# The local branch of a Mamba block: turned by transfers within SBUF, and projected by one matmul in place of four

## The chip, the cores and the metric

The kernel runs on one core of a Trainium2 chip, in one launch. The metric is device time in microseconds. Engines are named as in the profile: PE is TensorE (PEld its weight loads), DVE is VectorE, ACT is ScalarE, POOL is GpSimd, SP is SyncE, which in this kernel issues DMAs and nothing else. All data are 32-bit floats.

## The reference

The input is 32 images of 128 channels and 56 x 56 pixels. Layer 0 is a 7x7 depthwise convolution with a mixture of eight experts behind it. Layer 1, which the change touches, has a local and a global branch:

```python
xh = einsum('oi,bihw->bohw', cv1_w, x) + cv1_b
l  = depthwise_conv3x3(xh, dw_w)
l  = silu((l - bn_m) * (bn_g / sqrt(bn_v + 1e-5)) + bn_b)      # local branch, 128 channels
t  = layernorm_over_channels(tokens(xh))
g  = mamba(t)      # in_proj, causal conv, scan over 256 channels x 16 states, gate, out_proj
out = einsum('oi,bihw->bohw', cv2_w, concatenate([l, g], axis=1)) + cv2_b
return x + out
```

`cv2_w` is 128 x 256: its first 128 input channels take the local branch `l`, the others the global branch `g`.

## The kernel before

Layer 1 works on chunks of 448 pixels (8 image rows; seven chunks per image, 224 in all, numbered `g`). Within a chunk, the 16 states of the scan are 16 units. For each unit, GpSimd multiplies `du` by a broadcast row of B (`db_pool`, L1331), ScalarE makes the decay (`exp_act`, L1344), VectorE runs the scan over 2 x 449 columns (`scan_dve`, L1362 and L1366), VectorE or GpSimd multiplies by a broadcast row of C (`cmul`, L1382), and TensorE adds the product up in PSUM (`sum_pe`, L1285).

The rows of B and C (`bb` and `cb`) are loaded by `bc_load` (L1325), two units at a time and broadcast to 128 partitions, from a small DRAM tile `bc_d`, which `px_act` has stored there (L1189). `bb` and `cb` have three buffers each. All loads and stores of the layer are issued by SP, in one order.

That order, like that of every engine, is written out by hand. The table `PLAN` has a key for each step of a chunk and `UNITS` for each step of a unit. A key is a place in time counted in units, relative to the chunk's (or the unit's) own start; chunk `g` starts at 16 g. All steps of all chunks are sorted by key and emitted in that order, and each engine works through its own part of the list. A step can thus stand among the steps of the chunk before or after.

The local branch goes like this. `lt_pe` makes the 3x3 convolution in two PSUM tiles: TensorE works in 64 x 64 quarters, so channels 64 r to 64 r + 63 are in tile r, and within a tile the partitions 64 k to 64 k + 63 hold half k of the chunk's 448 columns. `lt_act` (L1266, keys -3.032 and -2.343) applies the batch norm and writes `lt`, 128 partitions x 2 (r) x 224 columns. `lt_silu` (L1171, key 2.033) applies SiLU in place. Much later `out_pe` (key 23.328, so among the steps of the next chunk) makes the output in one PSUM tile `p_out`: the residual `x1` through the identity (L1301), the local branch with `cvlt` (L1305), and the global branch with `wo` (L1311). Since `lt` has its channels spread over r and the partition half, `cvlt` is kept as four 128 x 128 matrices, one for each k and r, in which the half of the rows that belongs to the other k is zero; four matmuls over 224 columns each take the place of one plain one. `out_act` (L1316) and a store `out<-ot` follow.

`weights` loads all weights of layer 1 while layer 0 still works.

Of the kernel before, what the change touches and what calls it, by code (L numbers as in the profile page):

```python
# [5 lines left out]
F32 = mybir.dt.float32  # L6
# [7 lines left out]
C = 128  # L14
# [20 lines left out]
CH1 = L // NQ1  # L35
TPC1 = CH1 // TT
HD = 64
# [51 lines left out]
    (-2.343, "lt_act", 1),  # L89
    (2.033, "lt_silu"),  # L90
    (3.656, "dd_pe"),
    (18.599, "yz_dve", 0),
    (18.857, "yz_dve", 1),
    (23.328, "out_pe"),
# [150 lines left out]
def tile_kernel(tc: tile.TileContext, a: dict, out: bass.AP):  # L245
    nc = tc.nc
# [13 lines left out]
    with (  # L260
# [15 lines left out]
        for k in (HW - 1, 3 * HW - 1):  # L276
            nc.gpsimd.affine_select(
                out=perm, in_=perm, compare_op=ALU.not_equal, fill=1.0, base=-k, pattern=[[1, TT]],
# [7 lines left out]
        def column(v, name):  # L286
            t = const.tile([v.shape[0], 1], F32, name=name)
            nc.sync.dma_start(out=t, in_=v.unsqueeze(1))
            return t
# [185 lines left out]
        with (  # L475
# [9 lines left out]
            for k in range(0, E * CAP // 128, ZT):  # L485
# [6 lines left out]
                out=before, in_=ones[:, :128], compare_op=ALU.is_gt, fill=0.0, base=0,  # L492
# [7 lines left out]
            for q in range(QB):  # L500
                p = rp.tile([128, 3, TT], F32, name="p_turn", tag="tot", bufs=3)
# [61 lines left out]
            def total(v, first=None):  # L563

                p = rp.tile([128, v.shape[1]], F32, name="p_tot", tag="tot", bufs=3)
                if first is not None:
                    nc.tensor.matmul(p, lhsT=ones[:, :128], rhs=first, start=True, stop=False)
                nc.tensor.matmul(p, lhsT=ones[:, :128], rhs=v, start=first is None, stop=True)
                return p
# [22 lines left out]
            for h in range(2):  # L592
                p = total(cnts[h])
                r = room[:, h * HE : (h + 1) * HE]
# [33 lines left out]
            def chosen(i):  # L628
                t = tie[:, i, :]
                r = rs.tile([128, PT], F32, name="junk")  # L630
                nc.vector.tensor_tensor(
                    r.rearrange("j (r t) -> j r t", t=RUN), upto[:, i, :].rearrange("j (r t) -> j r t", t=RUN),
                    over[:, i, :].unsqueeze(2).to_broadcast([128, PT // RUN, RUN]), ALU.is_gt,
                )
                nc.vector.tensor_tensor(r, r, t, ALU.mult)
                nc.vector.scalar_tensor_tensor(
                    t, key[:, i, :], cands[i // HE][:, i % HE : i % HE + 1], r, ALU.is_gt, ALU.add
                )
                scan(i)
                return earlier(upto[:, i, PT - 1 : PT])  # L640
# [14 lines left out]
            p = chosen(0)  # L655
            for i in range(E):
                pn = chosen(i + 1) if i + 1 < E else None
                places(i, p)
                p = pn
# [15 lines left out]
        def weights(wp, wt, pw):  # L675
            def mm_tile(name):
                return pw.tile([128, 512], F32, name=name, tag="mm")
# [22 lines left out]
            dtt = wp.tile([128, DI], F32, name="dtt")  # L700
            nc.vector.memset(dtt, 0.0)
            nc.sync.dma_start(out=dtt[:DR], in_=a["dt_proj_wT"])
            cvlt = wp.tile([128, 2, 2, C], F32, name="cvlt")
            nc.gpsimd.memset(cvlt, 0.0)
            for k in range(2):
                nc.sync.dma_start(
                    out=cvlt[k * HD : (k + 1) * HD, k], in_=a["cv2_wT"][:C, :].rearrange("(r d) c -> d r c", r=2)
                )
            cv2b = column(a["L1_conv_cv2_b"], "cv2b")
            c1b3 = wp.tile([128, 2, 1], F32, name="c1b")  # L710
            turned(a["L1_conv_conv1d_b"].unsqueeze(1), c1b3)
# [41 lines left out]
            for h in range(2):  # L753
# [7 lines left out]
            p = mm_tile("p_mb")  # L761
# [11 lines left out]
                out=inp[:, 2:4, :], in_=a["L1_conv_in_proj_w"][DI:].rearrange("(h p) c -> p h c", p=128)  # L773
# [19 lines left out]
            p = mm_tile("p_ms")  # L793
# [8 lines left out]
            for k in range(DC + 1):  # L802
                p = mm_tile("p_wk")
                for h in range(2):
                    if k < DC:
                        s = wt.tile([128, C], F32, name="inx_s", bufs=2)
                        nc.vector.tensor_scalar_mul(s, inp[:, h, :], c1w[:, h, k : k + 1])
                    else:
                        s = inp[:, 2 + h, :]
# [5 lines left out]
            p = mm_tile("p_wo")  # L815
            for h in range(2):
                nc.tensor.matmul(
                    p[:, h * 128 : (h + 1) * 128], lhsT=wop[:, h * 128 : (h + 1) * 128], rhs=cvgt,
                    start=True, stop=True,
# [14 lines left out]
        with (  # L834
# [13 lines left out]
            for q in range(QB):  # L848
                for p0 in range(0, TT, XT):
                    ps = slice(p0, p0 + XT)  # L850
                    o = q * TT + p0
                    xgs = [dp.tile([128, XT, RW], F32, name=f"xg{k}") for k in range(2)]
                    nc.sync.dma_start(out=xgs[0][:, :, :C], in_=res_b[q, :, ps, :])
                    nc.scalar.copy(xgs[1][:, :, :C], xgs[0][:, :, :C])  # L854
                    for k, xg in enumerate(xgs):
                        nc.vector.tensor_copy(xg[:, :, C], gates[k][:, o : o + XT])  # L856
                        nc.vector.tensor_copy(xg[:, :, C + 1].bitcast(I32), backs[k][:, q, ps])
                        for j in range(XT):
                            apart(nc.gpsimd.indirect_dma_start(  # L859
                                out=buf_d[:, :],  # L860
                                out_offset=bass.IndirectOffsetOnAxis(ap=slots[k][:, o + j : o + j + 1], axis=0),
                                in_=xg[:, j, :], in_offset=None,
                            ), "scatter")
                if q == QB // 2:
                    w3 = weights(w3p, w3t, p3t)
# [5 lines left out]
        with (  # L871
# [8 lines left out]
                out=lsr, in_=a["L0_conv_layer_scale"].rearrange("c a b -> (c a b)").partition_broadcast(128)  # L880
# [47 lines left out]
            for e in range(E):  # L928
# [10 lines left out]
                for i0 in range(0, CAP, GT * 128):  # L939
# [3 lines left out]
                    for j, m, n in wholes(tiles):  # L943
                        r0 = e * CAP + i0 + j * 128
                        nc.sync.dma_start(
                            out=xb[:n, j:m, :],
                            in_=buf_d[r0 : r0 + (m - j) * n, :].rearrange("(k p) c -> p k c", p=n),
# [12 lines left out]
        with tc.tile_pool(name="p3", bufs=2, space=PSUM) as pmm:  # L960

            def mm_tile(name):
                return pmm.tile([128, 512], F32, name=name, tag="mm")

            layer1(w3 | locals())
# [3 lines left out]
def layer1(s):  # L969
# [3 lines left out]
    nc, tc, N = s["nc"], s["tc"], s["N"]  # L973
# [4 lines left out]
    st = [dict() for _ in range(G + 2)]  # L978
# [3 lines left out]
    with (  # L982
# [279 lines left out]
        def lt_act(g, r):  # L1262
            d = st[g]
            if r == 0:
                d["lt"] = two.tile([128, 2, CH1 // 2], F32, name="lt")
            nc.scalar.activation(  # L1266
                d["lt"][:, r, :], d["p_l"][r][:, : CH1 // 2], AF.Identity,
                bias=s["bnt"][:, r, 0:1], scale=s["bnt"][:, r, 1:2],
            )

        def yz_dve(g, h):
            d = st[g]
            if h == 0:
                d["yz"] = one.tile([128, 2, CH1], F32, name="yz")
            nc.vector.tensor_tensor(d["yz"][:, h, :], d["py"][:, h, :CH1], d["zs"][:, h, :], ALU.mult)
            if h == 1:
                del d["py"], d["zs"]
# [20 lines left out]
        def out_pe(g):  # L1298
            d = st[g]
            d["p_out"] = p = mm_tile("p_out")  # L1300
            nc.tensor.matmul(p[:, :CH1], lhsT=ident, rhs=d.pop("x1"), start=True, stop=False)  # L1301
            lt = d.pop("lt")
            for k in range(2):
                for r in range(2):
                    nc.tensor.matmul(  # L1305
                        p[:, k * CH1 // 2 : (k + 1) * CH1 // 2], lhsT=s["cvlt"][:, k, r, :], rhs=lt[:, r, :],
                        start=False, stop=False,
                    )
            yz = d.pop("yz")
            for r in range(2):  # L1310
                nc.tensor.matmul(p[:, :CH1], lhsT=s["wo"][:, r, :], rhs=yz[:, r, :], start=False, stop=r == 1)  # L1311
# [135 lines left out]
```

## Time and profile before

| | |
|---|---|
| median of 3 runs | 15727.1 us (15721.97 to 15732.7) |
| the profiled execution | 15731.48 us, of which its span is 15729.8 us |
| busy in the span: PE, PEld | 12850.2 us (82%), 7187.1 us (46%) |
| busy in the span: DVE, ACT, POOL | 11117.9 us (71%), 10499.4 us (67%), 13444.6 us (85%) |
| DMA | 2521.00 MB, mean 160 GB/s |

The span is the time from the first to the last instruction. Busy time is a mean over stages with different limits, so layer 1 has to be read by itself: it begins after about 5,700 us and lasts to the end. In a line of the timeline the first two numbers are the start in us from the span's start and the duration in us; a matmul of 32-bit floats leaves two records, each with its own weight load.

### The profile page before, as it was taken

Reading aid. Unit: us, or ns where it says so; the run is one execution under the profiler, and the core shown is the slowest. Engines: PE = TensorE matmul, PEld = TensorE weight load, DVE = VectorE, ACT = ScalarE, POOL = GpSimd, SP = SyncE. Lnnn points to the kernel's source line nnn. Section 1 sums busy time; section 2 is a strip of 40 time slices with the busy share of each in tenths; the row PEclk is TensorE's granted clock in tenths of the full one; section 3 lists DMA queues with packets and bytes.
Section 4 is the critical chain, followed back from the end, with each engine's and each line's share of the span. In section 5 each row is a group of like instructions: output and inputs, shape, how many; then the busy total and the mean of one; then the engine's idle time right before and its main releaser. Section 6 shows DMA issues by size and latency. Waiting matters only on the chain. (4 is left out here: it accounts for less than half of the span.)

```text
span 15729.8 us, 249821 instructions
## 1 busy us (share of the span) xinstructions
PE 12850.2 (82%) x92981; PEld 7187.1 (46%) x92981; DVE 11117.9 (71%) x11366; ACT 10499.4 (67%) x21038; POOL 13444.6 (85%) x8122
## 2 busy tenths in 40 slices
PE   7997200003999989999999999999999999999998
PEld 7996100002777754444444444444444444444443
DVE  2655500000111149999999999999999999999999
ACT  4564300001444458888888888888888888888887
POOL 2343377777888879999999999999999999999999
PEclk9997555556999999999999999999999999999999
DMA  8785422223555545555555555555555555555555
GB/s 264 231 234 167 186 78 78 78 78 69 71 70 72 70 106 183 184 185 182 182 184 182 183 184 184 181 183 182 183 184 183 181 184 183 182 185 185 179 183 167
DMA packets 1325298, 2521.00 MB, mean 160 GB/s; under 512 B 139352, under 2 KB 777136, under 8 KB 1316400
## 3 DMA queue, kind: packets, MB, share of 16 engines
q1 hardware_dynamic: 1127600, 2310.57, 47.2%
q0 software_dynamic: 196480, 194.45, 7.3%
q8 instruction: 732, 11.99, 0.3%
q14 instruction: 486, 3.98, 0.1%
HBM read 2129.06 MB, written 375.43 MB: 159 GB/s over the span
## 5 line engine op out<-in xcount | busy, mean ns | idle before, releaser
L1331 POOL TENSOR_TENSOR db<-du,bb 128x896 f32<-128x896 f32 x3584 | 6838.7, 1939 | 0.1
L1344 ACT ACTIVATE da<-dt,aneg 128x449 f32<-128x449 f32 x7168 | 4539.9, 637 | 389.1 <-DVE prod L1382 114.5
L1362 DVE TENSOR_TENSOR_SCAN da<-da,db 128x898 f32<-128x898 f32 x2240 | 4522.6, 2019 | 3.0 <-ACT da L1344 2.2
L1285 PE MATMUL py<-prod,ident 64*64 64x448 f32 x28672 | 3241.5, 548 | 174.6 <-DVE prod L1382 130.0
L1382 POOL TENSOR_TENSOR prod<-hs,cb 128x896 f32<-128x896 f32 x1344 | 2604.6, 1938 | 189.4 <-DVE r L1094 85.7
L1382 DVE TENSOR_TENSOR prod<-da,cb 128x896 f32<-128x896 f32 x2240 | 2438.7, 1089 | 199.0 <-DMA cb<-bc_d 85.2
L859 POOL DMA_INDIRECT buf_d<-xg,slot x1568 | 1515.4, 966 | 481.7 <-issue 453.9
L911 POOL DMA_INDIRECT res_d<-ys,xb x984 | 1587.8, 1614 | 332.3 <-issue 271.0
L1362 DVE TENSOR_TENSOR_SCAN hs<-da,db 128x898 f32<-128x898 f32 x896 | 1784.7, 2012 | 0.1
L1285 PEld LDWEIGHTS py<-prod,ident 64*64 64x64 f32 x28672 | 1018.0, 132 | 1628.2 <-issue 887.4
L951 PE MATMUL ept<-ident,xb 128*128 128x128 f32 (+1 forms) x984 | 188.7, 274 | 1916.7 <-DMA xb<-buf_d 1916.7
L1125 PE MATMUL p_xm<-te,wk 128*128 128x448 f32 x3584 | 1395.5, 540 | 0.0
L903 DVE TENSOR_TENSOR ys<-py,b2t 128x512 f32<-128x512 f32 (+2 forms) x256 | 170.7, 670 | 1690.5 <-PE py L897 1667.1
L856 DVE COPY xg<-gate 128x14 f32<-128x14 f32 x112 | 20.3, 184 | 1740.9 <-DMA buf_d<-xg,slot 1740.9
L854 ACT COPY xg<-xg 128x1792 f32<-128x1792 f32 x56 | 94.5, 1688 | 1684.3 <-DMA buf_d<-xg,slot 1673.4
L897 PEld LDWEIGHTS py<-w2t,hh 128*128 128x128 f32 x7872 | 936.2, 191 | 175.5 <-issue 113.4
L951 PEld LDWEIGHTS ept<-ident,xb 128*128 128x128 f32 (+1 forms) x984 | 124.6, 143 | 1920.1 <-issue 1919.8
L897 PE MATMUL py<-w2t,hh 128*128 128x128 f32 x7872 | 985.0, 278 | 0.3
L1125 PEld LDWEIGHTS p_xm<-te,wk 128*128 128x128 f32 x3584 | 671.5, 189 | 665.5 <-issue 567.1
L379 PE MATMUL pc<-xc,toep 112*112 112x112 f32 (+1 forms) x8192 | 944.9, 271 | 36.5 <-ACT toep L368 31.9
L1366 DVE TENSOR_TENSOR_SCAN hs<-da,db 128x449 f32<-128x449 f32 x896 | 926.2, 1076 | 1.4 <-ACT db L1390 0.8
L1257 PE MATMUL p_l<-xh,dwd 64*64 64x224 f32 x16128 | 907.1, 352 | 22.7 <-ACT dt L1239 4.2
(241 smaller groups left out, 20290.1 us busy)
## 6 DMA issues: line engine op xcount, KB each, us to landing
bb<-bc_d SPq DMA_DIRECT2D x1792, 448.0 KB
cb<-bc_d SPq DMA_DIRECT2D x1792, 448.0 KB
toep<-toep_d SPq DMA_DIRECT2D x448, 392.0 KB
buf_d<-zero SPq DMA_DIRECT2D x28, 2275.0 KB
xb<-buf_d SPq DMA_DIRECT2D x240, 260.0 KB
xt<-in_x SPq DMA_DIRECT2D x32, 1568.0 KB
res_d<-xa SPq DMA_DIRECT2D x128, 392.0 KB
xg<-res_d SPq DMA_DIRECT2D x56, 896.0 KB
```

The lines of the kernel that those rows point to most:

```text
L379: nc.tensor.matmul(pc[:, c, :, lo:hi], lhsT=tp[c // 2][:, c % 2, 6 - 2 * o : 8 - 2 * o, :], rhs=s4[:, c, :, lo + o - 1 : hi + o - 1], star ...
L859: apart(nc.gpsimd.indirect_dma_start(out=buf_d[:, :], out_offset=bass.IndirectOffsetOnAxis(ap=slots[k][:, o + j : o + j + 1], axis=0), in_ ...
L897: nc.tensor.matmul(py[:n, j, :], lhsT=hh[:, k, j * 128 : j * 128 + n], rhs=w2t[:, k, :], start=k == 0, stop=k == KF - 1,)
L911: apart(nc.gpsimd.indirect_dma_start(out=res_d[:, :], out_offset=bass.IndirectOffsetOnAxis(ap=xb[:n, j, C + 1 : C + 2].bitcast(I32), axis= ...
L1125: nc.tensor.matmul(p[:, :CH1], lhsT=s["wk"][:, k, hs], rhs=d["te"][:, k : k + CH1], start=k == 0, stop=k == DC - 1 and not first,)
L1257: nc.tensor.matmul(d["p_l"][r][k * HD : (k + 1) * HD, : CH1 // 2], lhsT=s["dwd"][rs, t, rs], rhs=d["xh"][rs, dy + k * R : dy + (k + 1) * R ...
L1285: nc.tensor.matmul(ps[r][h * HD : (h + 1) * HD, :CH1], lhsT=lhsT(rs, h), rhs=rhs[rs, h, :], start=start, stop=stop,)
L1331: nc.gpsimd.tensor_tensor(dbv[i][:, :, 1:], st[g]["du"], units[u].pop("bb"), ALU.mult)
L1344: e = nc.scalar.activation(da[:, h * W1 : (h + 1) * W1], st[g]["dt"][:, h, :], AF.Exp, scale=s["aneg"][:, h, i : i + 1])
L1362: nc.vector.tensor_tensor_scan(hs, da, dbs[i], 0.0, ALU.mult, ALU.add)
L1366: half(u, h, nc.vector.tensor_tensor_scan(hs2[h][:, hh], da[:, hh], dbs[i][:, hh], 0.0, ALU.mult, ALU.add))
L1382: eng.tensor_tensor(w["prod"], w["hs"][0][:, :, 1:], w["cb"], ALU.mult)
```

## The change

The step `lt_turn` is new, with key 5.0. Four DMAs, issued by SP, copy the quarters of `lt` into a new tile `lc` that has 128 channels as partitions and all 448 columns beside each other. `out_pe` then needs one matmul over 448 columns with the plain 128 x 128 `cvlt`. `lt` has one buffer in place of two; `lc` has two. The weight `cvlt` is loaded by one plain DMA, without a memset.

```diff
     (2.033, "lt_silu"),
     (3.656, "dd_pe"),
+    (5.0, "lt_turn"),
     (18.599, "yz_dve", 0),
...
-            cvlt = wp.tile([128, 2, 2, C], F32, name="cvlt")
-            nc.gpsimd.memset(cvlt, 0.0)
-            for k in range(2):
-                nc.sync.dma_start(
-                    out=cvlt[k * HD : (k + 1) * HD, k], in_=a["cv2_wT"][:C, :].rearrange("(r d) c -> d r c", r=2)
-                )
+            cvlt = load(a["cv2_wT"][:C, :], [C, C], "cvlt")
...
         def lt_act(g, r):
             d = st[g]
             if r == 0:
-                d["lt"] = two.tile([128, 2, CH1 // 2], F32, name="lt")
+                d["lt"] = one.tile([128, 2, CH1 // 2], F32, name="lt")
...
+        def lt_turn(g):
+            d = st[g]
+            lt = d.pop("lt")
+            lc = d["lc"] = two.tile([C, CH1], F32, name="lc")
+            for r in range(2):
+                for k in range(2):
+                    nc.sync.dma_start(
+                        out=lc[r * HD : (r + 1) * HD, k * CH1 // 2 : (k + 1) * CH1 // 2],
+                        in_=lt[k * HD : (k + 1) * HD, r, :],
+                    )
...
-            lt = d.pop("lt")
-            for k in range(2):
-                for r in range(2):
-                    nc.tensor.matmul(
-                        p[:, k * CH1 // 2 : (k + 1) * CH1 // 2], lhsT=s["cvlt"][:, k, r, :], rhs=lt[:, r, :],
-                        start=False, stop=False,
-                    )
+            lt = d.pop("lc")
+            nc.tensor.matmul(p[:, :CH1], lhsT=s["cvlt"], rhs=lt, start=False, stop=False)
```

`HD` is 64, `CH1` is 448 and `C` is 128. The lines of the profile before are those of the kernel before; in the changed kernel the matmul stands at L1310 and the new transfers at L1273.

## The prediction

> **What bounds the kernel now.** The diff touches the second layer, and beside that only a few instructions that run once, so I read the layer by itself: the windows view (columns: stretch and its length, then busy time and instruction count of each engine, granted TensorE clock, DMA share, GB/s).
>
> ```profile
> core 0: us, PE busy (x) PEld busy (x) DVE busy (x) ACT busy (x) POOL busy (x), PEclk, DMA share, GB/s
> 8000.00:10000.00 2000.00, 1908.12 (x14060) 895.80 (x14060) 1960.87 (x1530) 1729.96 (x3588) 1960.72 (x1049) 1.00 0.58 183
> ```
>
> VectorE and GpSimd are both busy 98% of the time and TensorE 95.4%. Ninety chunks pass in the 4000 us from 8000 to 12000 (90 `lt_silu` activations, L1171), so a chunk takes 44.4 us and 224 of them 9,950 us. Two engines at 98% can't both be read as the limit from busy time, so the waits come next, over the whole run (engine, line, what it waited for: us in total, times, longest). VectorE:
>
> ```profile
> DVE prod L1382 <- DMA cb<-bc_d: 85.2, 147, 2.1
> ...
> DVE yz L1275 <- PE py L1285: 4.0, 1, 4.0
> ...
> DVE prod L1382 <- PE p_var L1072: 3.1, 2, 1.6
> ```
>
> and GpSimd:
>
> ```profile
> POOL prod L1382 <- DVE r L1094: 85.7, 140, 1.1
> ...
> POOL prod L1382 <- DMA cb<-bc_d: 18.3, 30, 1.8
> POOL prod L1382 <- PE py L1285: 5.9, 28, 0.3
> ...
> POOL prod L1382 <- PE p_cv L1038: 4.0, 2, 2.1
> ```
>
> GpSimd waits once per chunk for VectorE (a scan whose product it takes; the named `r` stands beside it in VectorE's queue). Within the layer VectorE waits for other engines only in such single cases; what recurs is the load `cb`, 85.2 us in all. So VectorE with the `cb` loads sets the pace, and everything that TensorE ever makes these two wait is 4.0 + 3.1 + 5.9 + 4.0 = 17.0 us. Busy at 95%, TensorE is almost as full as the others and is still not waited for.
>
> Then the place of the change, in the timeline of SP's DMA queue in one chunk (start us, us, instruction). `lt_turn` (key 5.0) comes behind `px_act`'s store `bc_d<-xd` (16 - 11.507 = 4.493) and ahead of the next chunk's `bb` load of units 2 and 3 (18 - 11.504 = 6.496):
>
> ```profile
> 9008.09 1.79 SPq L1325 DMA_DIRECT2D cb<-bc_d  x2
> 9009.94 0.42 SPq L1189 DMA_DIRECT2D bc_d<-xd  x1
> 9015.23 0.32 SPq L1325 DMA_DIRECT2D bb<-bc_d  x1
> 9015.60 0.42 SPq L1015 DMA_DIRECT2D x<-in_x  x1
> 9016.08 0.43 SPq L1017 DMA_DIRECT2D yg<-res_d  x1
> 9020.90 0.32 SPq L1325 DMA_DIRECT2D cb<-bc_d  x1
> ```
>
> and all engines in the same microseconds:
>
> ```profile
> 9012.11 1.68 PE L1305 MATMUL p_out<-lt,cvlt 128*128 128x224 f32 x8
> ...
> 9012.57 2.01 DVE L1362 TENSOR_TENSOR_SCAN da<-da,db 128x898 f32<-128x898 f32 x1
> ...
> 9013.62 1.67 PE L1311 MATMUL p_out<-yz,wo 128*128 128x448 f32 x4
> ...
> 9014.67 1.09 DVE L1382 TENSOR_TENSOR prod<-da,cb 128x896 f32<-128x896 f32 x1
> ```
>
> The queue stands still from 9010.36 to 9015.23, 4.87 us, because `bb` reads what `bc_d<-xd` is still writing. The same place is also where VectorE is tightest: the product at 9014.67 needs the `cb` load issued at 9009.56, two DMAs ahead of the new ones. The trace's semaphore records put the landing of that load 4.43 us (median of 140 chunks; 3.2 to 6.5) after the issue of `bc_d<-xd`, about 9014.4; the scan ends at 9014.58. There is 0.2 us to spare.
>
> **The change, part by part.**
> *TensorE.* Four matmuls over 224 columns go: L1305 has 8 records (two per matmul), 1.68 us per chunk. One matmul over 448 columns comes; the row L1311 has two of exactly that shape, 1.67 us, so one is 0.83. TensorE loses 1.68 - 0.83 = 0.85 us per chunk, 190 us in all. What of that is on the path: at most the 17.0 us above, at least nothing; I take nothing, since those are single waits of 0.2 to 4 us and not a steady one. If all of it counted, the time would be 190 us less. At the end of the program `p_out` is in the chain that ended last, so the last chunk's 0.85 us count in full. The new matmul waits for four transfers issued 45 us before (`out_pe` of a chunk runs one chunk after its `lt_turn`).
>
> *SP's queue.* Four more issues per chunk, at 0.42 us as L1189, L1015 and L1017 (longest L1189 issue 1.43): 1.7 us, at most 5.7, beginning at 9010.4. The 4.87 us pause covers the first; past it, `bb`, `x`, `yg` and the next `cb` would shift, by 0.9 us at most. The `cb` at 9020.90 waits 4.4 us for GpSimd after `yg` is issued, so even that is covered. Their own waits are past: `lt_silu` ended at 9001.07, and the `lc` buffer was last read by the `out_pe` of 44 us ago. What the new ones are put ahead of is also used late: `bb` of units 2 and 3 by `db_pool` at key 15.71 (9.2 units of 44.4/16 = 2.78 us, 25 us, after its own key), `x` and `yg` by `moe_pe` 6.8 units (19 us) after theirs.
>
> *ScalarE.* `lt` has one buffer in place of two, so the next chunk's `lt_act` (9028.48) now waits for the transfers. Issued by 9012.1 and behind stores that land at 9014.6 (median; worst 9016.6), they should land by about 9017, with `out<-ot` (224 KB, 4.0 us) as nearest row. Ten us to spare: nothing. If that cover went, ScalarE would stand still with the next `exp_act` behind it, and VectorE after that.
>
> *DMA engines.* 4 x 56 KB = 224 KB more per chunk. A chunk moves 16 x 448 + 3 x 224 + 56 = 7,896 KB now, so 2.8% more. At 183 GB/s for a share of 0.58, the engines do 315 GB/s when busy, so 224 KB cost 0.73 us; with packets of 896 B in place of 3,584, I allow up to double, 1.46 us. That falls into the pause: after the `cb` load and `bc_d<-xd` have drained there is no other traffic until `bb` is issued. Does it slow the `cb` load ahead of it? In all 140 chunks no part of `bc_d<-xd` landed before the first part of that `cb` load, though it was issued 0.37 us later: what is issued later waits its turn. So I take nothing, and keep as upper end that the `cb` load is stretched by the whole 0.73 to 1.46 us. A gain here is excluded: no transfer is removed.
>
> There is a rule that speaks against the edit. The Trainium skill (SBUF — State Buffer, sections "Door 1: The DMA port swizzle" and "The DMA setup-cost knee") says that a transfer over 64 partitions reaches half of the SBUF ports, 196 GB/s against 328 at 1 MiB, that each transfer pays about 2 us, and that one transfer over 128 partitions should be used rather than several. No row here shows a 64-partition transfer between SBUF tiles. By the page's figures, and with the fixed parts one after the other, an estimate is 4 x 2 + 1.2 = 9.2 us per chunk, landing near 9020: beyond the pause, still 8 us before `lt_act`, and the sum would be the same.
>
> *Once per run.* A GpSimd memset of 0.6 us (L704) and one of two weight DMAs go, in a stage where GpSimd issues scatters: -0.6 us at most.
>
> *Sum.* The profiled execution took 15731.5 us (span 15729.8 and 1.7 around it): -0.85 at the end, -0.6 at the weights, 0 in the layer (between -17 and, by the slower rival, +282) give 15730. The median of the runs is 4.4 us under the profiled one: 15726.
>
> **The rivals.** *Nothing changes* (forecast): 15726, between 15,705 (all 17 us of waits for TensorE go) and 15,757 (+0.2%).
>
> *Slower: the new transfers stretch the `cb` load in front of them.* For it: only 0.2 us to spare at 9014.67, DMA engines full from 9009 to 9013, and VectorE is the pace, so what it waits there is not made up. Against it: the order of landings above. Price: 0.73 to 1.46 us less 0.2 to spare, 0.5 to 1.26 us on 224 chunks, +119 to +282 us, 15,845 to 16,008; stretched by 0.4 us, +45, 15,771. It decides from 0.14 us per chunk (31 us / 224) beyond the spare time.
>
> *Faster: a bound on TensorE that the waits don't name.* For it: 95.4% busy, with backlogs of five units of sums behind `out_pe`. Against it: the 17.0 us. Up to 190 us, 15,536. With that goes a milder case: the `cb` waits (85.2 + 18.3 = 103.5 us) move with the new timing of the queue and half of them vanish, -52, 15,674.
>
> *`lt_act` waits for its single buffer*: would need a landing 10 us late; 2%, counted with slower.
>
> **How the numbers follow.** About 0.2%, 31 us, is what a measurement of this kernel can tell from no change. No change within that: 0.64. Slower by the stretched load: 0.21, with the single buffer 0.23. Faster: 0.13, of which 0.08 is the milder case. The range goes from 15,674 (leaving out the 5% of the strong TensorE case and part of the milder one) to 15,845 (leaving out the upper half of the slower one); the likeliest case's own range is 15,705 to 15,757.
>
> **What would show it.** Right: four new issues between `bc_d<-xd` and `bb` with `bb` still 5.3 us after `bc_d<-xd`; L1310 at 0.83 us per chunk; TensorE busy some 1.9% less of the layer, with VectorE and GpSimd at 98% as before; "DVE prod <- DMA cb" near 85 us; no wait of ScalarE's `lt` for `lc`. Wrong: that `cb` wait at 130 us or more (slower rival); a chunk under 44.3 us with the `cb` wait unchanged (TensorE did bind); `bb` issued a microsecond or more later with a wait behind it.

## The result: slower by 0.45%, and the profile after

The changed kernel takes 15798.25 us (median of 5, 15788.62 to 15804.6) against 15721.97 us for the kernel before (median of 5: the three runs given above and two more). The ratio is 1.0045, 95% interval 1.0033 to 1.0056: 76 us, or 0.34 us for each of the 224 chunks. The profiled execution after has a span of 15786.9 us, 57.1 us more than before. This lies in the range, not at the forecast "no change" but between the mild case of the slower rival (15,771) and the lower end of its price (15,845).

The layer by itself, in the windows view after:

```profile
core 0: us, PE busy (x) PEld busy (x) DVE busy (x) ACT busy (x) POOL busy (x), PEclk, DMA share, GB/s
8000.00:10000.00 2000.00, 1876.01 (x13737) 837.08 (x13737) 1948.85 (x1521) 1719.31 (x3564) 1948.18 (x1041) 1.00 0.58 187
```

All engines are less busy per microsecond, VectorE and GpSimd too (98.0% to 97.4%): these two have their old work and more idle time. What VectorE waits for, over the whole run:

```profile
DVE prod L1384 <- DMA cb<-bc_d: 143.3, 193, 2.9
...
DVE prod L1384 <- PE p_var L1068: 19.0, 23, 1.0
```

The first row was 85.2 us and 147 times; 130 us or more was the prediction's sign for the slower rival. The second row was 3.1 us, and it names TensorE, but nearly all of these waits end as a `cb` load lands too: of 172.3 us of idle time ahead of VectorE's products (stretches over 0.15 us), 164.5 end within 0.15 us after such a landing. Together the two rows grow by 74.0 us. The layer, from the first to the last `lt_silu`, grows by 69.0 us (9925.2 to 9994.2). The span grew by only 57.1 us, since in the profile after layer 1 began 9.4 us earlier and the stretch behind the last `lt_silu` was 2.5 us shorter. SP's queue in one chunk after:

```profile
9019.45 1.79 SPq L1327 DMA_DIRECT2D cb<-bc_d  x2
9021.29 0.42 SPq L1185 DMA_DIRECT2D bc_d<-xd  x1
9021.77 2.39 SPq L1273 DMA_DIRECT2D lc<-lt  x4
9027.11 0.33 SPq L1327 DMA_DIRECT2D bb<-bc_d  x1
```

and VectorE in the same microseconds:

```profile
9023.93 2.01 DVE L1364 TENSOR_TENSOR_SCAN da<-da,db 128x898 f32<-128x898 f32 x1
9026.96 1.09 DVE L1384 TENSOR_TENSOR prod<-da,cb 128x896 f32<-128x896 f32 x1 [1.02 <-DMA cb<-bc_d]
```

The four issues lie in the pause as forecast, and `bb` still follows `bc_d<-xd` by 5.30 us in the median, as before (by 5.8 us in the chunk shown). But the product that the prediction found tightest now stands still, here for 1.02 us, for the `cb` load of units 8 and 9, the second of the two issued just ahead of the transfers. Each DMA of SP leaves 16 semaphore records in the trace, read here as one for each part that has landed; the last one is taken as its landing. In chunks 60 to 199, that load's landing after the issue of `bc_d<-xd` went from 4.43 us to 4.92 us (medians); it is issued at the same point, 0.37 us ahead of `bc_d<-xd`. Below, "the landing" means this number.

The same records show what this does to VectorE, chunk by chunk. The time to spare at this product, from the load's landing to the end of the scan ahead of the product, was 0.08 us before and is -0.41 us after (medians); the load came too late in 53 of the 140 chunks before and in 107 after. VectorE's idle time ahead of the product grew from 0.312 to 0.635 us on average. Over the whole layer, those idle stretches ahead of VectorE's products that end within 0.15 us after the landing of this load add up to 54.9 us before and 138.0 us after. Below, they are called "the waits for this load".

TensorE got its relief. In the groups of the window 8000 to 12000, with 89 chunks in it,

```profile
L1310 PE MATMUL p_out<-lc,cvlt 128*128 128x448 f32 x178 | 81.5, 539 | 0.0
```

is 0.92 us per chunk (81.5 us over 89 chunks) where four matmuls took 1.68.

### The profile page after: what moved, and what is told of

It is laid out like the page before. It is cut to its first block, busy times and chain, and to the rows that moved or that the text cites. A ratio compares the mean times of both kernels' runs of the same rounds, so it can differ in the third digit from the quotient of the medians.

```text
span 15786.9 us, 248931 instructions
## 1 busy us (share of the span) xinstructions
PE 12729.6 (81%) x91637; PEld 6897.9 (44%) x91637; DVE 11119.9 (70%) x11366; ACT 10506.2 (67%) x21038; POOL 13449.3 (85%) x8121
## 5 line engine op out<-in xcount | busy, mean ns | idle before, releaser
L1292 PE MATMUL py<-prod,ident 64*64 64x448 f32 x28672 | 3305.7, 551 | 340.0 <-DVE prod L1384 297.1
L1392 ACT COPY db<-da 128x2 f32<-128x2 f32 x1920 | 291.1, 162 | 972.9 <-DVE prod L1384 942.3
```

The lines of the kernel that those rows point to most:

```text
L1292: nc.tensor.matmul(ps[r][h * HD : (h + 1) * HD, :CH1], lhsT=lhsT(rs, h), rhs=rhs[rs, h, :], start=start, stop=stop,)
```

## The experiments

The experiments ran on three chips whose level differs (the kernel before: 15905 us with e1 to e4, 15724 us with e5 to e7 and b1, 15923 us with b2, b3 and e8). So of the times only ratios to the kernel before on the same chip are compared. A landing is the median of one trace; the two kernels without transfers and without the swap, on two chips, differ by 0.08 us (4.43 and 4.35 us in e2). Diffs that write code in short form are marked so.

**e1: the transfers without TensorE's relief** (diff in short form).

```diff
-            nc.tensor.matmul(p[:, :CH1], lhsT=s["cvlt"], rhs=lt, start=False, stop=False)
+            for k in range(2):
+                for weight in (s["cvlt"], zero_w):
+                    nc.tensor.matmul(p[:, half k], lhsT=weight, rhs=lt[:, half k], start=False, stop=False)
```

> The changed kernel with TensorE's old amount of work: the local branch again takes four matmuls over 224 columns, two with the plain weights and two with zeros, and the four transfers stay. Theory 1 (the transfers stretch the cb load issued just ahead of them): as slow as the changed kernel, 15,790 to 15,810 us, VectorE's waits for cb near 143 us, and that load landing near 4.9 us after the issue of bc_d<-xd. Theory 2 (the shorter out_pe moves the sums and VectorE's waits come from that): back to 15,715 to 15,735 us and cb waits near 85 us.

Measured: 15969.0 us, ratio 1.0038 (1.0024 to 1.0052); landing 4.90 us. VectorE's waits:

```profile
DVE prod L1391 <- DMA cb<-bc_d: 156.7, 213, 2.3
```

As slow as the changed kernel, within the intervals, with TensorE's old work. The loss comes with the transfers.

**e2: the matmul without the transfers** (diff in short form).

```diff
         def lt_turn(g):
-            ... four transfers from lt to lc
+            st[g].pop("lt")
+            st[g]["lc"] = lcs[g % 2]        # a tile of zeros
```

> The changed kernel without its transfers: the one matmul reads a tile of zeros, so the local branch is left out of the output. Theory 1 (stretched cb load): as before, 15,710 to 15,735 us, cb waits near 85 us, landing near 4.4 us; the 0.85 us per chunk that TensorE saves give nothing. Theory 2 (TensorE's new timing): stays at 15,790 to 15,805 us. If TensorE did bind a little, the time falls below 15,700 us.

Measured: 15904.46 us against 15904.79, ratio 1.0000 (0.9991 to 1.0009); landing 4.35 us; VectorE's `cb` waits:

```profile
DVE prod L1380 <- DMA cb<-bc_d: 69.7, 89, 1.9
```

The work that TensorE saves is worth nothing that can be measured, and theory 2 falls.

**e3: the transfers behind `yg`.**

```diff
-    (5.0, "lt_turn"),
+    (7.0, "lt_turn"),
```

> The changed kernel with key 7.0 in place of 5.0 for the transfers: SP issues them behind the loads bb, x and yg, some 6.6 us after bc_d<-xd, when the tight cb load has landed. Theory 1 (stretched cb load): 15,715 to 15,740 us, cb waits 80 to 95 us, landing near 4.4 us. Rival (the cost lies in SP's issues, the 24 DMAs per chunk or the added waits wherever they stand): stays at 15,785 to 15,810 us.

Measured: 15883.72 us, ratio 0.9984 (0.9975 to 0.9993); landing 4.32 us.

```profile
DVE prod L1384 <- DMA cb<-bc_d: 49.0, 90, 1.8
```

The same four issues, the same 24 DMAs per chunk and the same waits cost nothing when they start 6.67 us and not 0.47 us after `bc_d<-xd`, so it is the place that costs. That this kernel is a little faster than before was not expected; it is taken up at the end.

**e4 and e5: fewer bytes at the same place.** In e4 each transfer takes 8 of the 224 columns, in e5 112 (diff in short form: `cols` is 8 or 112).

```diff
-                        out=lc[r * HD : (r + 1) * HD, k * CH1 // 2 : (k + 1) * CH1 // 2],
-                        in_=lt[k * HD : (k + 1) * HD, r, :],
+                        out=lc[r * HD : (r + 1) * HD, k * CH1 // 2 : k * CH1 // 2 + cols],
+                        in_=lt[k * HD : (k + 1) * HD, r, :cols],
```

> The changed kernel with the same four transfers over the same 64 rows each, but 8 of the 224 columns (32 B a row in place of 896); the rest of the local branch stays zero. If the cb load is stretched by the bytes moved: 15,715 to 15,735 us, landing near 4.4 us. If it is stretched by the number of DMAs or rows that are handed to the DMA engines: 15,780 to 15,805 us, landing near 4.9 us. The packet sizes of the two traces speak for the second: the packets of the cb loads thin out from 1.5 us after bc_d<-xd, before the packets of 896 B start in number.

> The changed kernel with the same four transfers at key 5.0 over 112 of the 224 columns: half the bytes, 448 B a row; the other half of the local branch stays zero. If the cb load ahead is stretched in proportion to the bytes: landing about half way between 4.36 us (8 columns) and 4.92 us (all columns) after the issue of bc_d<-xd, 4.55 to 4.75, and a time half way between those two kernels, 1.000 to 1.003 of the time before. If only transfers beyond some size collide: as with 8 columns, 0.998 to 0.999.

Measured: e4 15880.61 us, ratio 0.9984 (0.9975 to 0.9993), landing 4.36 us; e5 15748.89 us, ratio 1.0011 (1.0002 to 1.0021), landing 4.66 us. With all 224 columns it is 1.0045 and 4.92 us. VectorE's `cb` waits in e4 and e5:

```profile
DVE prod L1386 <- DMA cb<-bc_d: 52.4, 99, 1.8
```

```profile
DVE prod L1386 <- DMA cb<-bc_d: 98.4, 179, 2.6
```

The landing grows with the bytes, +0.30 us for the first half and +0.26 us for the second, at an equal number of DMAs and rows. With the bytes grows the length of a row; the two were not separated. The reading of packet sizes that spoke for the number of DMAs was wrong.

**e6 and e7: which side of the transfer.** e6 moves the same bytes in the same 256 rows with two DMAs over all 128 partitions; e7 writes them to DRAM, and its matmul reads zeros (only the new lines of the transfers are shown).

```diff
# e6
+            for r in range(2):
+                nc.sync.dma_start(out=lc[:, r * CH1 // 2 : (r + 1) * CH1 // 2], in_=lt[:, r, :])
# e7
+            lc = s["dram2"].tile([C, CH1], F32, name="lc_d")
```

> The same 224 KB in the same 256 rows of 896 B at key 5.0, but as two transfers over all 128 partitions in place of four that go from one half of the partitions to one half; the channels are not turned, so the local branch of the output is permuted. If the stretch comes from the bytes that the engines move: as the changed kernel, 1.004 to 1.006 of the time before, landing 4.8 to 5.0 us. If it comes from writing to half of the partitions at a time: landing 4.35 to 4.55 us and 0.998 to 1.001 of the time before.

> The same four transfers at key 5.0 write to a DRAM tile and not to SBUF (the matmul reads zeros, so the local branch is left out). They read SBUF as before but write nothing into it. If the cb load ahead is held up by the new writes into SBUF: landing 4.35 to 4.5 us, 0.998 to 1.001 of the time before. If it is held up by the reads or by the DMA engines' own time: landing 4.75 us or later, 1.003 or more.

Measured: e6 15770.47 us, ratio 1.0030 (1.0018 to 1.0041), landing 4.84 us; e7 15772.66 us, ratio 1.0032 (1.0019 to 1.0044), landing 4.74 us. VectorE's `cb` waits in e6 and e7:

```profile
DVE prod L1379 <- DMA cb<-bc_d: 120.0, 207, 2.1
```

```profile
DVE prod L1387 <- DMA cb<-bc_d: 120.9, 207, 2.2
```

Both keep most of the loss, so neither the half partitions nor the writes into SBUF are the main part of it. That they are a little cheaper than the changed kernel (0.0013 to 0.0015, with intervals that overlap) is not settled. e6 also misses its expected 1.004 to 1.006, and e7's landing its expected 4.75 us or later, by 0.01 us.

**e8: the transfers ahead of both `cb` loads.**

```diff
-    (5.0, "lt_turn"),
+    (4.4, "lt_turn"),
```

> The changed kernel with key 4.4 for the transfers: they are issued ahead of the two cb loads. Queue order theory (what stands ahead costs its whole time, what stands behind only a part): the last cb load lands 0.7 us or more later than without transfers, cb waits of 250 us or more, 1.008 to 1.015 of the time before. If it makes no difference whether they stand just ahead or just behind: 1.004 to 1.006.

Measured: 16272.87 us, ratio 1.0221 (1.0207 to 1.0235), more than expected. VectorE's waits and SP's queue:

```profile
DVE prod L1384 <- DMA cb<-bc_d: 414.2, 242, 3.3
```

```profile
9045.62 0.32 SPq L1327 DMA_DIRECT2D bb<-bc_d  x1
9046.04 2.38 SPq L1273 DMA_DIRECT2D lc<-lt  x4
9048.52 1.03 SPq L1327 DMA_DIRECT2D cb<-bc_d  x2
9049.65 0.38 SPq L1185 DMA_DIRECT2D bc_d<-xd  x1
```

The expectation counted only the transfers. SP also needs 2.38 us to issue them: from `bb` to `bc_d<-xd` it is 4.03 us here. In the kernel before it was 2.26 us, with the store at 9009.94 and

```profile
9007.68 0.32 SPq L1325 DMA_DIRECT2D bb<-bc_d  x1
```

So both loads start late. That is nearly the whole cost. The transfers have all landed 0.63 us after `bc_d<-xd` is issued, before the first part of the last `cb` load lands (3.36 us), and from its own issue to its landing that load takes 4.98 us here, 4.80 in the kernel before and 5.29 in the changed kernel (medians). So it is not shown that what stands ahead costs a load its whole transfer time; here it cost the time that SP took to issue it, while the same bytes just behind lengthened the load itself. The place in the queue decides: 2.2% just ahead, 0.45% just behind, nothing three DMAs further on.

**b1: the kernel before, with the tight load first** (the key stands in the table of unit 8).

```diff
-        (-3.514, "bc_load", "cb"),
+        (-3.6, "bc_load", "cb"),
```

> The kernel before, with the key of unit 8's cb load moved from -3.514 to -3.6, so that the load of units 8 and 9 is issued ahead of that of units 10 and 11 and takes the buffer that comes free 1.5 us earlier. If VectorE's pace is set by the landing of this load: its wait about 5 us after bc_d<-xd goes, cb waits fall from 85 to 30 to 50 us and the time to 0.995 to 0.998 of that before. If another bound stands right behind (GpSimd, or the load of units 4 and 5): 0.999 to 1.001.

Measured: 15675.31 us against 15724.11, ratio 0.9968 (0.9956 to 0.9980).

```profile
DVE prod L1382 <- DMA cb<-bc_d: 29.7, 59, 1.9
```

Before, the load of units 10 and 11 was issued first and took the buffer that came free first, though VectorE needs units 8 and 9 first. Swapped, VectorE's `cb` waits fall by 55.5 us (85.2 to 29.7) and the time by 49 us. The waits for this load fall from 54.9 to 0.9 us. This one wait cost the kernel before about 49 us.

**b3 and b2: the same swap in the changed kernel**, with the transfers at 5.0 (b3) and at 7.0 (b2).

> The changed kernel, transfers at key 5.0 as they were, with the key of unit 8's cb load at -3.6: the load that the transfers stretch is then that of units 10 and 11, which VectorE takes some 6 us later. If the loss of the changed kernel is wholly VectorE's wait for that one load: 0.996 to 0.998 of the time before, as the kernel before with the same swap (0.9968), although the load right ahead still lands near 4.9 us. If the transfers cost anything elsewhere as well: 1.000 or more.

> Both repairs at once: the transfers behind yg (key 7.0) and unit 8's cb load first. Neither the loads nor TensorE should then hold VectorE about 5 us after bc_d<-xd: 0.995 to 0.997 of the time before. If it is faster than the swap alone (0.9968) by more than 0.1%, the single matmul has some worth after all; if equal, it has none.

Measured: b3 15872.82 us, ratio 0.9969 (0.9957 to 0.9981); b2 15869.76 us, ratio 0.9968 (0.9956 to 0.9980). In b3 the load right ahead of the transfers still lands late, at 4.63 us against 4.19 in b1, but it is now the load of units 10 and 11, and

```profile
DVE prod L1384 <- DMA cb<-bc_d: 33.3, 55, 1.9
```

says that VectorE no longer waits for it; the waits for the load of units 8 and 9 come to 5.9 us, against 138.0 in the changed kernel. The whole loss is gone, at key 5.0 and with every transfer in place. The fastest version is the swap, and with it the four matmuls and the one matmul are equal. b1 beats both kernels of this study: 0.9968 of the one, and by that some 0.8% below the changed one.

## Why the prediction was wrong, step by step

- *What bounds the kernel*: right. VectorE with the `cb` loads sets the pace (b1), and the tightest product was the right one. The 0.2 us to spare was too much: it set the median landing of 140 chunks against the scan's end in one chunk. In that chunk the load landed at 9014.52, 0.06 us ahead of the scan's end, and over the 140 chunks the median is 0.08 us, with the load already late in 53. The prediction's own row, 147 waits for `cb`, said that there was nothing to spare in many chunks. (Its GpSimd row counts 140 waits in 224 chunks, so not one per chunk.)
- *TensorE*: right, its relief is worth nothing (e2; b1 and b3 equal). It is 0.76 us per chunk, not 0.85, since the one matmul takes 0.92 us and not 0.83. The forecast's lower end of 15,705 should read 15,709 by its own sum (15,726 less 17.0); nothing hangs on it.
- *SP's queue* and *ScalarE*: right. The pause held the four issues (2.39 us in the chunk shown, between the 1.7 and 5.7 given), and ScalarE shows no wait of `lt` for the transfers.
- *DMA engines*: this is the step that failed. It said that a load issued earlier is not slowed by transfers issued later, since no part of `bc_d<-xd` landed before the first part of the `cb` load. That compared the first parts. A load is done when its last part has landed, and between its first and last landing (3.38 and 4.43 us) later transfers were already running: `bc_d<-xd` had its first part down at 3.56. After the change the first part of the transfers lands at 3.97 us and the last of the `cb` load at 4.92. The zero in the sum should have been about 0.32 us per chunk, the growth of VectorE's idle time at this product (0.635 less 0.312): times 224 that is 72 us, against 69 us for the layer in the two profiles and 76 us in the medians of the times.
- *The price of the slower rival* was bounded by 0.73 to 1.46 us of stretch; 0.49 us came, so the transfers cost the load ahead only a part of their own time. The mild case named there (0.4 us, 15,771) was the nearer one; it is too low because it takes off 0.2 us to spare in every chunk. The rival's 0.21 was too little: with hardly any slack and 0.7 us of traffic right behind, "nothing" needed a stronger reason.
- The Trainium skill (DMA: Bandwidth & Descriptors, section "Queues, rings and completion order") says that a DMA is split over up to 16 engines, each of which takes its work in order, and that completion is not in order of issue. The landings above agree for the parts: those of the transfers begin to land while parts of the load are still out. As a whole, though, the load, the store and the four transfers landed in order of issue in all 140 chunks.
- Of the rule on half the partitions and several transfers, e6 (two DMAs over 128 partitions) shows 4.84 us in place of 4.92: a small part at most. The estimate of 9.2 us made from it was too long: the last transfer landed 5.7 us after the first was issued (6.15 less 0.47), so four fixed parts of 2 us did not follow one another here.

## What to carry to other kernels

A transfer in a pause of the queue is not free for the load in front of it. Before calling it hidden, compare, chunk by chunk, the last landing of what is in flight with the moment at which its reader needs it; if less is to spare than the new traffic takes, move the transfer a few DMAs on, where here it cost nothing. And when one engine's only recurring wait is for one load, look first at which load is issued first: changing one key gave more (0.3%) than four matmuls turned into one.

## What the hardware did that was not expected

Queue order did not protect the load ahead: 224 KB issued 0.8 to 2.6 us after it made it land 0.49 us later. Half the bytes gave 0.30 us of the 0.56 us between 8 and 224 columns, and against the same 4.43 us before the stretch was still 0.31 us when the bytes went to DRAM (e7) and 0.41 us over all partitions (e6). By which part of the DMA engines this happens was not separated.

e3 and e4 are 0.16% faster than the kernel before (some 25 us), while e2 without any transfer is equal to it. That goes with the waits for the same load: 25.1 us in e3 and 29.4 in e4, against 54.9 in the kernel before and 54.2 in e2. In e3 and e4, late landings are rarer: the slowest tenth of landings begins at 4.77 us (e3) and 4.88 us (e4), against 5.38 us in the kernel before and in e2. In the kernel before, landings with an instruction fetch in flight (59 of the 140) average 4.79 us and others 4.33 us; in e3 4.42 and 4.26. That the fetches delay the load is not shown, and why late landings are rarer in e3 and e4 stays open.
